# Queries and new keys of a paged attention turned by VectorE and spread by SBUF transfers, with two projections inside the output projection

## The chip, the core and the metric

The kernel runs on one core of a Trainium2 chip. A core has five engines with an instruction queue each: TensorE (PE: matmuls and, beside them, weight loads, PEld), VectorE (DVE), ScalarE (ACT), GpSimd (POOL) and SyncE (SP), which computes nothing and issues transfers. Sixteen DMA engines move what SP, ACT and POOL issue. The metric is the time of one execution in microseconds (us). The kernel before took 2267.02 us, the median of three runs (2259.68, 2267.02 and 2267.82).

## The reference, cut to what matters

There are 64 batches of 32 tokens with 512 features, all in float32. First each batch is mixed by one of 16 small matrices; then comes an attention with 32 query heads and 8 key heads of 128 features, over 512 cached keys (16 pages of 32 through a block table) and the 32 new keys.

```python
x = x + einsum('bct,bcd->bdt', x, weights[condition])
q = rope(rmsnorm((x @ Wq.T).reshape(64, 32, 32, 128)) )   # k likewise with 8 heads, v without
k_all, v_all = concat(cache[block_table], new)            # 512 + 32 keys
scores = q @ k_all / sqrt(128), masked past cache_seqlens
out = x + softmax(scores) @ v_all @ Wo.T
```

## The kernel before

**Tiles and steps.** Four batches make a tile of 128 tokens, so there are `NT` = 16 tiles. The heads are done in two halves (`NHH` = 2) of 4 key heads and 16 query heads. A step is one half of the heads of one tile: 32 steps, 0 to 15 for the first half (the text calls them first-half steps) and 16 to 31 for the second. The first half computes the mixed tile x1, turns it and stores it to memory with the partial result; the second half loads both again (`x1_a`, L337 to L345). `ahead` is the step after the one in work: its projections are made during the step in work.

**Slots.** A step runs over 4 batches times 4 key heads, that is 16 slots (`slot = bt * GH + g`, L864). A slot holds `scores` of this head (8 weight loads and matmuls of a 128 x 512 block, L534, then an exponential on ACT, L542) and `values` of the head before (L592), whose results DVE adds to the part of the new keys and divides (L604, L606, L607). At slot 0 stand `new_scores` (L545) and at slots 1 and 3 `new_values` (L562). At slot 3 stands the output projection of the step before, `out_proj` (L475), 16 matmuls of 128 x 512 after all slots of that step have gone through DVE's `turn` (L614). Which pieces for `ahead` stand in which slot is the table `pieces` (L822): `x1_a` at 0, the key projection `k_a` and the first query projection at 4, and so on.

**Projection, norm and turn.** `project` (L394) makes four matmuls for a 128 x 512 block. `norm_rope` (L402) squares it on ACT, sums on DVE, takes the power -0.5 on POOL, and multiplies and adds on DVE up to L433. The block then has tokens on the partitions, but the scores need features there, so `transposed` (L438) turns it by four TensorE transposes into PSUM, and ACT copies it out (`q_b`, L466; `k_b`, L451).

**Cached keys and values.** `load_k` (L272) brings the keys of one batch: SP first loads the 16 page numbers into registers (L278) and then issues 16 transfers of 64 KB (L286). There are two buffers, so the load for the batch two ahead waits until `head_keys` (L521) has copied the last head out of the buffer. `head_keys` is a DVE copy (L527), one a slot, a batch ahead of its use. Values come by indirect transfers of POOL (L310), four a batch, and ACT masks them (L323).

**Order.** SP and PE run their instructions in the order of the program (`manual_schedule`, L88). The order of DVE, ACT and POOL is set at build time by a planner, which goes by readiness in its own model. Every engine waits at the head of its queue. On SP this order is: the load for the batch two ahead at the top of each batch (slots 0, 4, 8 and 12), then what the pieces of the slots issue; at slot 0 of a step with a second-half `ahead` these are `acc` and `x1t` (L343, L345), behind the key load of slot 0. The buffer of `x1t` is single, and so is that of `nv`, the part of the new keys.

Of the kernel before, what the change touches and what calls it, by code (L numbers as in the profile page):

```python
# [11 lines left out]
F32 = mybir.dt.float32  # L12
# [7 lines left out]
P = 128  # L20
# [35 lines left out]
def cond_resid_paged_attention_kernel(  # L56
# [64 lines left out]
    sin = const.tile([P, NT, HD], F32, tag="sin", name="sin")  # L121
    half_pi = const.tile([P, 1], F32, tag="half_pi", name="half_pi")
    minus_half = const.tile([P, GH], F32, tag="minus_half", name="minus_half")
    rden = const.tile([P, NHH * NT * BT, GH], F32, tag="rden", name="rden")

    def positions():
        nc.vector.memset(half_pi, math.pi / 2)
# [58 lines left out]
    def steps_of(exact, pools):  # L186
# [15 lines left out]
        else:  # L202
# [10 lines left out]
        ]  # L213
        vn_bufs = [
            wpool.tile([P, GH, D + 1], F32, tag=f"vn{i}", name=f"vn{i}_{uid}")
            for i in range(2)
        ]

# [112 lines left out]
        class Step:  # L331
            def __init__(self, n):
                self.n, self.hh, self.t = n, n // NT, n % NT
                self.name = f"{n}_{uid}"
                self.qt = {}

        def x1_a(st):  # L337

# [60 lines left out]
                )  # L399
            return pp  # L400

        def norm_rope(st, pp, name, kind):  # L402

            cw, sw = st.rot[kind]
            p4 = pp.rearrange("p (h e f) -> p h e f", h=4, e=2)
            sq = work.tile([P, 4, D], F32, tag="w2", name=f"sq_{name}", bufs=1)
            nc.scalar.activation(  # L407
                sq.rearrange("p h d -> p (h d)"), pp, AF.Square, scale=1.0 / math.sqrt(D)
            )
            ms = small.tile([P, 4], F32, tag="ms", name=f"ms_{name}")  # L410
            nc.vector.tensor_reduce(ms, sq, AX.X, ALU.add)  # L411
            nc.vector.tensor_scalar_add(ms, ms, EPS)  # L412
            rs = small.tile([P, 4], F32, tag="rs", name=f"rs_{name}")
            nc.gpsimd.tensor_tensor(rs, ms, minus_half, ALU.pow)  # L414

            r = work.tile([P, 4, 2, HD], F32, tag="w1", name=f"rope_{name}")
            u = work.tile([P, 4, 2, HD], F32, tag="w2", name=f"ropeu_{name}", bufs=1)
            nc.vector.tensor_tensor(  # L418
                r.rearrange("p h e f -> p h (e f)"),
                pp.rearrange("p (h d) -> p h d", h=4),  # L420
                cw.rearrange("p e f -> p (e f)").unsqueeze(1).to_broadcast([P, 4, D]),
                ALU.mult,
            )
            for e in range(2):
                nc.vector.tensor_tensor(
                    u[:, :, e, :],
                    p4[:, :, 1 - e, :],
                    sw[:, e, :].unsqueeze(1).to_broadcast([P, 4, HD]),
                    ALU.mult,
                )  # L430
            nc.vector.tensor_tensor(r, r, u, ALU.add)
            rd = r.rearrange("p h e f -> p h (e f)")
            nc.vector.tensor_tensor(  # L433
                rd, rd, rs.unsqueeze(2).to_broadcast([P, 4, D]), ALU.mult
            )
            return rd

        def transposed(rd, name):  # L438
# [2 lines left out]
                nc.tensor.transpose(pt[:, h, :], rd[:, h, :], ident)  # L441
            return pt

        def k_a(st):
            if st.n > 1 or exact:
                rot_tables(st)
            name = f"k_{st.name}"
            pp = project(st, wt["k", st.hh, 0], f"pp_{name}")
            st.k_rope = norm_rope(st, pp, name, "k")

        def k_b(st):  # L451
            pt = transposed(st.k_rope, f"k_{st.name}")
            st.kn = act.tile([P, GH, P], F32, tag="kn", name=f"kn_{st.name}")
            nc.scalar.copy(st.kn, pt)

        def v_a(st):
            pp = project(st, wt["v", st.hh, 0], f"pp_v_{st.name}")
# [2 lines left out]

        def q_a(st, g):
            name = f"q_{st.name}_{g}"
            pp = project(st, wt["q", st.hh, g], f"pp_{name}")
            st.qt[g] = norm_rope(st, pp, name, "q")

        def q_b(st, g):  # L466
            pt = transposed(st.qt[g], f"q_{st.name}_{g}")
            qt = act.tile([P, BT, REP, S], F32, tag=f"qt{g}", name=f"qt_{st.name}_{g}")
            nc.scalar.copy(  # L469
                qt.rearrange("p b h s -> p h b s"),  # L470
                pt.rearrange("p h (b s) -> p h b s", b=BT),
            )
            st.qt[g] = qt

        def out_proj(st, halfway=None):  # L475

            po = ps_p.tile([P, HID], F32, tag="pp", name=f"pout_{st.name}")
            for i in range(QH):
                if halfway and i == 3 * QH // 4:
                    halfway()  # L480
                nc.tensor.matmul(  # L481
                    po,
                    st.ot[:, i, :],
                    wt["o", st.hh, i // 4][:, i % 4, :],
                    start=(i == 0),
                    stop=(i == QH - 1),
                )
            nc.vector.tensor_tensor(st.acc, po, st.acc, ALU.add)  # L488
            if exact or st is steps[-1]:
                store(st)  # L490
# [25 lines left out]
                    mask_ones(self.b)  # L516

        def queries(ba, g):
            return ba.st.qt[g][:, ba.bt].rearrange("p h s -> p (h s)")

        def head_keys(ba, g, eng=None):  # L521

# [22 lines left out]
        def new_scores(st):  # L545


            ps = ps_p.tile([P, GH, P], F32, tag="pp", name=f"psn_{st.name}")
            for g in range(GH):
                for bt in range(BT):  # L550
                    own = slice(bt * S, (bt + 1) * S)
                    nc.tensor.matmul(  # L552
                        ps[own, g, :],
                        st.kn[:, g, own],
                        st.qt[g][:, bt].rearrange("p h s -> p (h s)"),
                        start=True,
                        stop=True,
                    )
            st.pn = work.tile([P, GH, P], F32, tag="pn", name=f"pn_{st.name}", bufs=1)
            nc.scalar.activation(st.pn, ps, AF.Exp, scale=SCALE)  # L560
# [25 lines left out]
        def values(ba, g):  # L586
# [14 lines left out]
            if g % 2:  # L601
                both = slice(g - 1, g + 1)
                t = ba.st.nv[:, ba.bt, both, :]
                nc.vector.tensor_tensor(t, ba.po, t, ALU.add)  # L604
                rd = rden[:, ba.n, both]
                nc.vector.reciprocal(rd, t[:, :, D])  # L606
                nc.vector.tensor_tensor(  # L607
                    ba.o[:, both, :],
# [14 lines left out]
        def exact_batch(ba, key_no):  # L623
# [7 lines left out]
            for g in range(GH):  # L631
# [6 lines left out]
                nc.tensor.matmul(  # L638
                    ps[:, L:LK],
                    q,  # L640
                    st.kn[:, g, bt * S : (bt + 1) * S],
                    start=True,
                    stop=True,
                )
# [41 lines left out]
        if exact:  # L686
# [7 lines left out]
            for st in steps:  # L694
# [10 lines left out]
                x1_a(st)  # L705
                x1_c(st)
                x1_b(st)
                k_a(st)
                k_b(st)
                v_a(st)  # L710
# [39 lines left out]
        lens_at = work.tile([P, B], I32, tag="pr", name="lens_at", bufs=3)  # L750
        nc.gpsimd.dma_start(lens_at, lens_row.partition_broadcast(P))
        positions()
        trig = work.tile([P, 3, TRIG * HD], F32, tag="w1", name="trig0")
        angles(0, trig)
        for i in range(BT):
            blk = slice(i * S, (i + 1) * S)
# [9 lines left out]
        cached_rows(pages_at, lens_at)  # L766
        nc.vector.memset(vn_bufs[0][:, :, D : D + 1], 1.0)
        nc.vector.memset(vn_bufs[1][:, :, D : D + 1], 1.0)
        trig = work.tile([P, 3, TRIG * HD], F32, tag="w1", name="trig1")
        angles(TRIG, trig)  # L770
        for c in range(RAW):
            fetch(0, c)
# [49 lines left out]
        def pieces(st):  # L822
            do = {
                0: (x1_a,),
                4: (k_a, (q_a, 0)),
                5: ((q_a, 1),),
                6: (v_a, k_b, (q_b, 0)),
                8: ((q_a, 2), (q_b, 1)),
                10: ((q_a, 3), (q_b, 2)),
                13: ((q_b, 3),),  # L830
            }
            if st is second:
                do[4], do[6] = ((q_a, 0),), (k_b, (q_b, 0))
            return do

        valued, turned = (batch, GH - 1), batch
        new_ot(first)
# [14 lines left out]
        for st in steps:  # L852
# [4 lines left out]
            for bt in range(0 if st.n else 1, BT):  # L857
# [5 lines left out]
                for g in range(GH):  # L863
# [16 lines left out]
                    if slot == 3:  # L880
                        if ahead:
                            x1_b(ahead)
                        out_proj(steps[st.n - 1])
                        if st.n + 1 < NT // TRIG:
                            tmp = work.tile([P, 3, TRIG * HD], F32, tag="w1", name=f"trig_{st.n}")
                            with tc.issue_after(last["dve"]), tc.issue_after(last["act"]):
                                angles((st.n + 1) * TRIG, tmp)
                    if slot == 5 and st.n:
                        store(steps[st.n - 1])
                    if slot == 6 and 0 < st.n and st.n + 2 < NT:  # L890
# [25 lines left out]


        def in_range():
            rd = rden.rearrange("p n g -> p (n g)")
            good = work.tile([P, NHH * NT * BT * GH], F32, tag="w1", name="good")  # L920
            nc.vector.tensor_scalar(good, rd, DEN_LOW, None, ALU.is_ge)
            nc.vector.scalar_tensor_tensor(good, rd, DEN_HIGH, good, ALU.is_le, ALU.mult)
            count = small.tile([P, 1], F32, tag="ms", name="count")
            nc.vector.tensor_reduce(count, good, AX.X, ALU.add)
            ones = small.tile([P, 1], F32, tag="rs", name="ones")
            nc.vector.memset(ones, 1.0)
            pc = ps_p.tile([1, 1], F32, tag="pp", name="pcount")
            nc.tensor.matmul(pc, count, ones, start=True, stop=True)
            nc.vector.tensor_scalar(
                redo, pc, float(P * NHH * NT * BT * GH), None, ALU.not_equal  # L930
            )

        out_proj(steps[-1], in_range)

    redo = const.tile([1, 1], I32, tag="redo", name="redo")
    run(False)
# [54 lines left out]
```

## Time and profile before

| | |
|---|---|
| median of three runs | 2267.02 us |
| profiled execution, its own time | 2258.59 us |
| its span, first to last instruction | 2256.8 us |
| granted TensorE clock, mean | 0.997 |
| busy PE / PEld / DVE / ACT / POOL | 2223.5 / 1565.7 / 1076.0 / 940.4 / 779.8 us |
| DMA moved | 318.13 MB, mean 141 GB/s |
| TensorE transposes of queries and keys (L441) | 640 matmuls |
| issues of cached keys on SP (L286) | 2048 |

The page gives a busy time for each engine and a row for each group of equal instructions; a busy engine is not always the bound, and only the chain of work that ended last says what set the end. SP computes nothing, and so has no busy row; its issues are read from its timeline. In the text, s is the start of slot 0 of a step on PE.

### The profile page before, as it was taken

What the parts mean: (1) busy time and instruction counts of PE and PEld (TensorE: products, weight loads), DVE (VectorE), ACT (ScalarE), POOL (GpSimd) and SP (SyncE); (2) the same over time, 40 slices, a digit from 0 to 9 for tenths busy, and PEclk for the clock granted to TensorE, in tenths of its full rate; (3) what the DMA queues carried; (4) which work ended last, traced back from release to release, by engine and by line L of the source; (5) the groups of instructions that cost most, each with busy time, mean ns of one, the idle gap of its engine ahead of it and who ended that gap; (6) DMA issues with size and microseconds to landing.
All of it is one profiled execution on the core that took longest, in us unless ns stands there. A gap on an engine that the chain in (4) does not pass through costs nothing.

```text
span 2256.8 us, 41920 instructions
## 1 busy us (share of the span) xinstructions
PE 2223.5 (99%) x13590; PEld 1565.7 (69%) x13590; DVE 1076.0 (48%) x2722; ACT 940.4 (42%) x1724; POOL 779.8 (35%) x1008
## 2 busy tenths in 40 slices
PE   8999999999999999999999999999999999999998
PEld 5767677676776677766777666777666777666775
DVE  5545455443554444543545544455444455444452
ACT  3534454444433444433444333443334443343442
POOL 4423333233433333332333333333323343233331
PEclk9999999999999999999999999999999999999999
DMA  7744544345443455435756444553344544444542
GB/s 229 195 131 128 154 134 128 114 128 154 142 121 113 130 152 155 116 113 157 229 168 169 124 137 138 154 148 115 115 145 139 160 124 127 124 130 151 159 116 74
DMA packets 364053, 318.13 MB, mean 141 GB/s; under 512 B 46800, under 2 KB 308960, under 8 KB 363824
## 3 DMA queue, kind: packets, MB, share of 16 engines
q1 hardware_dynamic: 319104, 174.44, 27.0%
q0 software_dynamic: 41712, 136.66, 20.4%
q10 hardware_dynamic: 3008, 4.25, 0.5%
q8 instruction: 110, 1.80, 0.3%
q14 instruction: 119, 0.97, 0.1%
HBM read 302.59 MB, written 12.58 MB: 140 GB/s over the span
## 4 chain that ended last, share of the span: by engine, by line
PE 90%; DMA 4%; DVE 2%; issue 2%; SPq 2%; ACT 1%; POOL 1%; ACTq 0%; DVEq 0%; POOLq 0%
PE pout_x L481 19%; PE pp_q_x L397 19%; PE po_x L592 18%; PE ps_x L534 18%; PE pp_k_x L397 5%; PE pp_v_x L397 5%; PE pt_q_x L441 2%; PE pnv_x L576 2%; DMA raw_x<-in_vc_dram,v_row 2%; SPq L286 1%; PE psn_x L552 1%; DMA k_t_x<-in_kt_dram 1%; PE pt_k_x L441 1%; PE pmix_x L353 1%; DMA pages_at<-in_pages_v_dram 0%
## 5 line engine op out<-in xcount | busy, mean ns | idle before, releaser
L310 POOL DMA_INDIRECT raw_x<-in_vc_dram,v_row x512 | 515.0, 1006 | 718.6 <-ACT v_x L323 659.3
L542 ACT ACTIVATE pr_x<-ps_x 128x512 f32<-128x512 f32 x512 | 305.4, 600 | 628.3 <-PE ps_x L534 624.8
L592 PE MATMUL po_x<-v_x,pr_x 128*128 128x129 f32 x4096 | 551.9, 278 | 5.6 <-ACT pr_x L542 5.6
L534 PE MATMUL ps_x<-qt_x,kh_x 128*128 128x128 f32 x4096 | 542.1, 275 | 2.8 <-DVE kh_x L527 2.2
L592 PEld LDWEIGHTS po_x<-v_x,pr_x 128*128 128x128 f32 x4096 | 503.1, 192 | 49.5 <-issue 30.4
L534 PEld LDWEIGHTS ps_x<-qt_x,kh_x 128*128 128x128 f32 x4096 | 502.8, 192 | 27.3 <-issue 19.8
L397 PE MATMUL pp_q_x<-wq_x,x1t_x 128*128 128x512 f32 x1024 | 463.7, 596 | 3.3 <-ACT qt_x L469 3.3
L481 PE MATMUL pout_x<-wo_x,ot_x 128*128 128x512 f32 x1024 | 445.0, 592 | 0.0
L323 ACT ACTIVATE v_x<-raw_x,valid 128x512 f32<-128x512 f32 x512 | 362.6, 724 | 114.4 <-DMA raw_x<-in_vc_dram,v_row 113.9
L481 PEld LDWEIGHTS pout_x<-wo_x,ot_x 128*128 128x128 f32 x1024 | 192.2, 190 | 229.0 <-issue 228.7
L397 PEld LDWEIGHTS pp_q_x<-wq_x,x1t_x 128*128 128x128 f32 x1024 | 188.4, 192 | 203.8 <-issue 200.1
L527 DVE COPY kh_x<-k_t_x 128x512 f32<-128x512 f32 x506 | 213.2, 424 | 108.8 <-DMA k_t_x<-in_kt_dram 68.2
L407 ACT ACTIVATE sq_q_x<-pp_q_x 128x512 f32<-128x512 f32 x128 | 76.4, 597 | 306.5 <-issue 135.4
L411 DVE TENSOR_REDUCE ms_q_x<-sq_q_x 128x4 f32<-128x512 f32 x128 | 87.4, 682 | 200.0 <-ACT sq_q_x L407 200.0
L414 POOL TENSOR_TENSOR rs_q_x<-ms_q_x,minus_half 128x4 f32<-128x4 f32 x128 | 132.9, 1038 | 132.7 <-DVE ms_q_x L412 132.7
L604 DVE TENSOR_TENSOR nv_x<-po_x,nv_x 128x258 f32<-128x258 f32 x256 | 107.7, 421 | 146.9 <-PE po_x L592 138.7
L386 POOL TENSOR_TENSOR cw_k_x<-norm_k,cos 128x64 f32<-128x64 f32 x32 | 10.1, 315 | 382.7 <-DVE ms_k_x L412 382.7
L418 DVE TENSOR_TENSOR rope_q_x<-pp_q_x,cw_q_x 128x512 f32<-128x512 f32 x128 | 87.3, 682 | 103.4 <-PE pt_k_x L441 103.4
L488 DVE TENSOR_TENSOR xt_x<-pout_x,xt_x 128x512 f32<-128x512 f32 x16 | 11.1, 692 | 246.6 <-PE pout_x L481 246.6
L488 DVE TENSOR_TENSOR acc_x<-pout_x,acc_x 128x512 f32<-128x512 f32 x16 | 11.1, 692 | 220.7 <-PE pout_x L481 220.7
L397 PE MATMUL pp_v_x<-wv_x,x1t_x 128*128 128x512 f32 x256 | 115.2, 593 | 0.0
L397 PE MATMUL pp_k_x<-wk_x,x1t_x 128*128 128x512 f32 x256 | 115.2, 593 | 0.0
(99 smaller groups left out, 1575.7 us busy)
## 6 DMA issues: line engine op xcount, KB each, us to landing
k_t_x<-in_kt_dram SPq DMA_DIRECT2D x2048, 64.0 KB
raw_x<-in_vc_dram,v_row POOLq DMA_INDIRECT x512, 4.0
wo_x<-in_wo_dram SPq DMA_DIRECT2D x32, 256.0 KB
xt_x<-in_x_dram SPq DMA_DIRECT2D x16, 256.0 KB
x1t_d<-x1t_x ACTq DMA_DIRECT2D x16, 256.0 KB
acc_d<-xt_x SPq DMA_DIRECT2D x16, 256.0 KB
wq_x<-in_wq_dram SPq DMA_DIRECT2D x8, 512.0 KB
acc_x<-acc_d SPq DMA_DIRECT2D x16, 256.0 KB
```

Of the source, the lines that this page charges most:

```text
L310: nc.gpsimd.indirect_dma_start(out=raw.rearrange("p g d -> p (g d)"), out_offset=None, in_=vc, in_offset=bass.IndirectOffsetOnAxis(ap=v_ro ...
L323: nc.scalar.activation(v_bufs[b % 2][:, c, :, 0:D], raw, AF.Copy, scale=ok)
L397: nc.tensor.matmul(pp, st.x1t[:, c, :], w[:, c, :], start=(c == 0), stop=(c == KC - 1))
L411: nc.vector.tensor_reduce(ms, sq, AX.X, ALU.add)
L414: nc.gpsimd.tensor_tensor(rs, ms, minus_half, ALU.pow)
L418: nc.vector.tensor_tensor(r.rearrange("p h e f -> p h (e f)"), pp.rearrange("p (h d) -> p h d", h=4), cw.rearrange("p e f -> p (e f)").uns ...
L481: nc.tensor.matmul(po, st.ot[:, i, :], wt["o", st.hh, i // 4][:, i % 4, :], start=(i == 0), stop=(i == QH - 1),)
L527: last["dve"] = nc.vector.tensor_copy(k, ba.k_raw[:, :, g, :]).ins
L534: nc.tensor.matmul(ps[:, c, :], ba.k[g][:, c * P : (c + 1) * P], queries(ba, g), start=True, stop=True,)
L542: last["act"] = nc.scalar.activation(pr, ps, AF.Exp, scale=SCALE).ins
L592: nc.tensor.matmul(ba.po[:, g % 2, :], ba.pr[g][:, c, :], ba.v_t[:, c, g, :], start=(c == 0), stop=(c == VC - 1),)
L604: nc.vector.tensor_tensor(t, ba.po, t, ALU.add)
```

## The change

The queries and new keys are no longer turned by TensorE after step 0. `turn_rows` has DVE transpose the blocks of 32 x 32, which leaves each block's features on the 32 partitions of its batch; the piece `spread` then has SP issue 16 transfers within SBUF (4 batches times 4 blocks of features, each 32 partitions of 2560 bytes) that bring each block to its own partitions. The queries and keys of a step lie together in `rows`; each transfer takes all five of them and so waits for the last query. The columns of batches 0 to 2 have one buffer, those of batch 3 have two. The projections of the keys and of the first query group now stand inside the output projection, after its 4th and its 8th matmul; the other projections move up in the slots. The tables of the rotation are made at slot 2. The check of the denominators (`rden`) is made once for each half of the heads. The buffer `w1` becomes single.

```diff
+        rows = wpool.tile([P, 4, GH + 1, P], F32, tag="rows", name=f"rows_{uid}")
+        q_cols = wpool.tile([P, BT - 1, GH + 1, P], F32, tag="q_cols", name=f"q_cols_{uid}")
+        q_last = [
+            wpool.tile([P, GH + 1, P], F32, tag=f"q_last{i}", name=f"q_last{i}_{uid}")
+            for i in range(2)
+        ]
...
+        def turn_rows(st, i, rd, name):
+            nc.vector.transpose(
+                rows[:, :, i, :].rearrange("p k (h s) -> p h k s", h=4),
+                rd.rearrange("p h (k d) -> p h k d", k=4),
+            )
+        def columns(st, bt):
+            return q_last[st.n % 2] if bt == BT - 1 else q_cols[:, bt]
+        def spread(st, batches):
+            for bt in batches:
+                for k in range(4):
+                    nc.sync.dma_start(
+                        columns(st, bt)[k * S : (k + 1) * S, :, :],
+                        rows[bt * S : (bt + 1) * S, k, :, :],
+                    )
+        def by_tensor(st):
+            return st.n == 0 or exact
+        def finish(st, i, pp, name, kind):
+            if by_tensor(st):
+                norm_rope(st, pp, name, kind, rows[:, :, i, :])
+            else:
+                turn_rows(st, i, norm_rope(st, pp, name, kind), name)
+        def to_columns(st, i):
+            pt = transposed(rows[:, :, i, :], f"{i}_{st.name}")
+            p4 = pt.rearrange("p h (b s) -> p b h s", b=BT)
+            n = BT - 1
+            nc.scalar.copy(q_cols[:, :, i, :].rearrange("p b (h s) -> p b h s", h=4), p4[:, 0:n])
+            nc.scalar.copy(
+                columns(st, n)[:, i, :].rearrange("p (h s) -> p h s", h=4), p4[:, n]
+            )
...
-        def out_proj(st, halfway=None):
+        def out_proj(st, between={}):
             po = ps_p.tile([P, HID], F32, tag="pp", name=f"pout_{st.name}")
             for i in range(QH):
-                if halfway and i == 3 * QH // 4:
-                    halfway()
+                if i in between:
+                    between[i]()
...
         def queries(ba, g):
-            return ba.st.qt[g][:, ba.bt].rearrange("p h s -> p (h s)")
+            return columns(ba.st, ba.bt)[:, g, :]
...
             do = {
                 0: (x1_a,),
-                4: (k_a, (q_a, 0)),
-                5: ((q_a, 1),),
-                6: (v_a, k_b, (q_b, 0)),
-                8: ((q_a, 2), (q_b, 1)),
-                10: ((q_a, 3), (q_b, 2)),
-                13: ((q_b, 3),),
+                2: (rot_tables,),
+                4: ((q_a, 1),),
+                5: (v_a,),
+                6: ((q_a, 2),),
+                8: ((q_a, 3),),
+                10: ((spread, (0, 1, 3)),),
+                11: ((spread, (2,)),),
             }
...
                     if slot == 3:
                         if ahead:
                             x1_b(ahead)
-                        out_proj(steps[st.n - 1])
+                        between = {}
+                        if ahead:
+                            between[REP] = lambda: k_a(ahead)
+                            between[2 * REP] = lambda: q_a(ahead, 0)
+                        out_proj(steps[st.n - 1], between)
...
+                    if slot == GH and st.n == NT:
+                        count(0)
```

## The prediction

> **What bounds the kernel now.** I read the page's busy shares first, then the chain that ended last, then one step of it (the second-half step that begins at 1571.95), and at last the queues of SP, DVE and ACT in that step.
>
> ```profile
> PE 2223.5 (99%) x13590; PEld 1565.7 (69%) x13590; DVE 1076.0 (48%) x2722; ACT 940.4 (42%) x1724; POOL 779.8 (35%) x1008
> ...
> PE 90%; DMA 4%; DVE 2%; issue 2%; SPq 2%; ACT 1%; POOL 1%; ACTq 0%; DVEq 0%; POOLq 0%
> ```
>
> TensorE is the bound nearly everywhere; what leaves it is gained, and what makes it wait is lost. The chain prices the work that leaves:
>
> ```profile
> 1567.05 0.44 PE pt_q_x L441 x4
> ...
> 1580.26 1.31 PE pnv_x L576 x15
> 1581.57 1.09 PE po_x L592 x8
> 1582.66 13.73 PE pout_x L481 x32
> ```
>
> Four transposes (with their four loads) take 0.437 us. The third line's wait is small but telling: the same `pnv` takes 0.66 us elsewhere. Its cause is seen on DVE and ACT:
>
> ```profile
> 1574.98 0.43 DVE L604 TENSOR_TENSOR nv_x<-po_x,nv_x 128x258 f32<-128x258 f32 x1 [3.35 <-PE po_x L592]
> 1578.55 0.43 DVE L527 COPY kh_x<-k_t_x 128x512 f32<-128x512 f32 x1 [3.14 <-DMA k_t_x<-in_kt_dram]
> ...
> 1579.09 0.42 DVE L607 TENSOR_TENSOR o_x<-nv_x,rden 128x256 f32<-128x256 f32 x1
> ...
> 1579.60 1.21 ACT L584 COPY nv_x<-pnv_x 128x258 f32<-128x258 f32 x4 [3.07 <-DVE o_x L607]
> ```
>
> The key copy waits 3.14 us at the head of DVE for a late key load; behind it the old `nv` is read late, so ACT may not overwrite it, the PSUM tiles of `new_values` stay full, and PE waits 0.65 us. So key loads already arrive at the limit at the start of a step. SP says why:
>
> ```profile
> 1549.18 9.26 SPq L286 DMA_DIRECT2D k_t_x<-in_kt_dram  x16
> ...
> 1565.55 9.66 SPq L286 DMA_DIRECT2D k_t_x<-in_kt_dram  x16
> ...
> 1585.56 0.43 SPq L343 DMA_DIRECT2D acc_x<-acc_d  x1
> 1586.09 0.38 SPq L345 DMA_DIRECT2D x1t_x<-x1t_d  x1
> ```
>
> The loads of slots 8 and 12 each need over 9 us of SP to issue; the load of slot 0 follows at once (first issue 1576.55, after its 1.0 us load of page numbers, L278) and ends at 1585.5; only then comes `x1t`. One issue costs SP about 0.52 us, gap included, also where the address is fixed and 32 partitions are moved:
>
> ```profile
> 1211.65 4.05 SPq L239 DMA_DIRECT2D wo_x<-in_wo_dram  x8
> ```
>
> (4.05 - 0.43) / 7 = 0.52. The only pause of SP near here is 1558.4 to 1565.55, before the load of slot 12.
>
> **What the Trainium skill says.** "DMA: Bandwidth & Descriptors", section "Issuing engines are not separate DMA queues", calls the sequencer's time to initiate a DMA "usually small relative to the DMA itself". Here it isn't: 16 issues of 64 KB take 8.3 us, so SP brings at most 1.05 MB / 8.3 us = 126 GB/s this way. "SBUF — State Buffer", section "Door 1: The DMA port swizzle", measures 189 GB/s for 32 partitions, an estimate of 1.31 MB / 189 = 6.9 us for the spread, less than its issue time; no trace of before has such a transfer. "TensorE: Matmul & The Clock Gate", Part 1, halves the clock after an idle window of about 3.4 us. The start of this trace agrees: after PE's gap from about 25 to 29 us the granted clock falls.
>
> ```profile
> 24.00:28.00 4.00, 0.89 (x5) 1.00 1.02 380
> 28.00:32.00 4.00, 3.00 (x4) 0.68 1.05 391
> 32.00:36.00 4.00, 4.00 (x19) 0.89 0.78 245
> ```
>
> (Columns: stretch and its length, PE busy, clock, DMA share, GB/s.) One such gap costs 4 x 0.32 + 4 x 0.11 = 1.7 us.
>
> **The change, part by part.**
>
> *Gain on PE.* Transposes go in 31 of 32 steps: 31 x 5 x 0.437 = 67.7 us, 2.18 us a step. The projections only move; their 3.44 us each stay.
>
> *DVE.* 155 block transposes at the 0.71 us of `turn`'s row (L617, same 128 x 512): 110 us on an engine at 48%, so hidden as work; its latency counts below. The write is strided, so 0.7 to 1.0 us. ACT loses 5 copies of 0.59 us a step, worth nothing as it waits 625 us for PE. Tables at slot 2, the single `w1`, and the two checks of `rden` (about 1 us of DVE each) are covered by PE's slots; uncovered they cost a microsecond once or so. Step 0 gains five more ACT copies, at most 2 us once.
>
> *When the rows are ready.* The last query projection now stands in slot 8. From its end to s are values (0.89) and seven slots of 1.79 us: 13.4 us. Its chain on ACT, DVE and POOL took 4.9 us in the step shown (projection end 1561.25 to the end of L433 at 1566.13); with 0.71 the rows are ready at s - 7.8.
>
> *The spread on SP.* 16 x 0.52 = 8.3 us, to s + 0.5 (bounds: 0.33 us for the instruction alone, 5.3 us; with the slow issues of the key loads at 0.6, 9.6 us). It cannot use SP's pause: slots 8 to 11 shrink to 10.6 us, the slot-8 load ends at about s - 8.4, and the rows come just then. The last transfer lands about 1.7 us after its issue (as `x1t` did: 1586.09 to the next issue, which waits for it, 1587.79), at s + 1.8; `new_scores` wants it at s + 0.9: a stall of 0.9.
>
> *What is behind it on SP.* The key load of slot 12 begins at s - 6.4 now (1565.55 against 1571.95). Behind the spread and the page load (1.3 with its gap) it begins at s + 1.9: 8.3 us later. Behind it, all 8.3 us later, are the load of slot 0 and `x1t`.
>
> - Second-half `ahead`, 16 steps: `x1t` was issued at s + 14.1, now at s + 22.4, and lands at s + 24.1. PE wants it after the fourth matmul of the output projection, no longer after the sixteenth: s + 10.1 (its start without the 0.65 stall) + 3.4 = s + 13.5. Stall 10.6; net 10.6 - 0.65 - 2.18 = +7.8 a step, +124 us.
> - The other 15 step starts: the key copy's wait ended at s + 5.3 in the first-half step that starts at 949.1, with 0.6 us to spare before PE; 8.3 later it stalls PE by 7.7, if DVE's order stays. The planner puts what it believes ready first, so it may put divisions and `turn` ahead of the late copy; then only the 0.9 remains. I take 6: the copy was planned at least 3.1 us too early in the step shown, so the planner is too sure of SP, and a copy behind the division still holds up the mix of x1 (`x1_c`). Net 6 - 2.2 = +3.8, +57 us (bounds +83 and -19).
>
> Sum: 2258.6 (the profiled execution's own time; span 2256.8) + 124 + 57 = 2440. That execution lies 8.4 us under the median and within the runs' 8 us of spread, more or less; I add half, 2445.
>
> **Rivals.**
> 1. *DVE re-planned.* The copies stand behind everything urgent; only `x1t` stalls: 2258.6 + 124 - 19 = 2364, with the offset 2370. For it: it needs no luck but the planner's. Against: the order of before.
> 2. *The clock falls too.* Stalls of 8 to 10 us are longer than the gap at 25 us; 31 x 1.7 = 53 on top of the fully blocked 2466: about 2520. For it: the clock row above. Against: waits may be broken into pieces by single slots.
> 3. *Faster: the spread fits into SP's pause.* If rows come early enough, or issues are cheap enough, that the slot-12 load begins at most x later, then second-half steps cost 1.8 + x - 2.83 (even unmoved, `x1t`, issued on average 3.0 us after the output projection began, comes 1.2 us after PE's new wish, 1.8 with the stall removed) and the others at most 0.9 - 2.2 or x - 0.6 - 2.2. Break-even is at x = 1.9 us; at x = 0 the time is 2258.6 - 16 - 19 = 2223, or 2230. For it: SP waits 663 us for key copies in all. Against: x is 8.3 by the rows, and even with all 16 issued at the bare 0.33 it is 5.3.
> 4. *DMA or DVE as the bound.* 1.31 MB on some 9.9 MB a step; slices up to 229 GB/s are on the page, and DVE would be at about half. No time of its own.
>
> **Chances.** Likeliest case (`x1t` and part of the DVE stalls, 2400 to 2500): 0.58; rival 1 and things near it (2330 to 2400): 0.23; rival 2 (above 2500): 0.12; rival 3: 0.05; within 0.5% (a chance cancellation): 0.02. Half a per cent, about 11 us, is what a measurement of this kernel can tell from no change. So faster 0.05, same 0.02, slower 0.93. The range 2340 to 2525 leaves out the faster cases and the tails of rivals 1 and 2.
>
> **What would show it.** Right: in the changed profile SP shows two runs of 12 and 4 spread issues ending near s, PE waits inside the output projection before the key projection in steps 15 to 30 for `x1t` by about 10 us, and key copies on DVE wait over 8 us at a step's start; PE's share falls to some 88%; no L441 after step 0. Wrong: spread issues far below 0.5 us, rows ready long before the slot-8 load ends, or `x1t` landing before s + 15.

## The result, and the profile after

The changed kernel takes 2614.28 us (median; 2605.06 to 2621.94) where the kernel before takes 2267.31 beside it: a ratio of 1.1538, 95% interval 1.1488 to 1.1587. It is slower, as forecast, but by 347 us instead of 178, and 2614 lies outside the range of 2340 to 2525.

The page of the changed kernel, first the busy time of each engine, then the granted clock in 40 slices, then the chain that ended last by engine and by line:

```profile
PE 2285.0 (87%) x12970; PEld 1582.6 (60%) x12970; DVE 1184.9 (45%) x2881; ACT 886.7 (34%) x1586; POOL 768.8 (29%) x1008
...
PEclk9899999999999999998889889988999889988899
...
PE 64%; SPq 19%; DMA 8%; issue 5%; DVE 2%; ACT 0%; POOL 0%; ACTq 0%; another core or an unknown queue 0%; POOLq 0%; DVEq 0%
PE pout_x L520 15%; PE pp_q_x L406 15%; PE po_x L631 11%; PE ps_x L573 11%; SPq L296 10%; SPq L470 7%; PE pp_k_x L406 6%; PE pp_v_x L406 4%; DMA q_cols_x<-rows_x 3%; DMA x1t_x<-x1t_d 3%; PE psn_x L591 1%; SPq L288 1%; PE pnv_x L615 1%; DMA wo_x<-in_wo_dram 1%; DMA wq_x<-in_wq_dram 1%
```

TensorE issues 620 matmuls fewer (31 steps x 5 x 4 transposes), and yet its busy time rises from 2223.5 to 2285.0. Its share falls from 99% to 87%, and the clock line, all nines before, has eights: one near the start, the others from the middle on, where the second half of the heads begins. SP's issuing, 2% of the chain before, is 19% now.

From the busy times it can be worked out where the time went. Take busy time as the work of before plus what slower matmuls add, and the rest of the span as idle:

| | span | PE busy | PE idle | busy beyond the work |
|---|---|---|---|---|
| before | 2256.8 | 2223.5 | 33.3 | |
| after | 2617.3 | 2285.0 | 332.3 | 129.2 |

The work of after is 2223.5 - 67.7 = 2155.8 (the transposes at 0.437 us for four are gone), so 2285.0 - 2155.8 = 129.2 us of busy time go beyond the work. Then +299.0 idle, +129.2 slow matmuls and -67.7 transposes make +360.5, the difference of the spans; as the 129.2 is what was left over, this balance closes by itself. The record of the granted clock in the trace tests it: it holds 1.0 or 0.5 and nothing between, TensorE was busy for 232.7 us at 0.5, and half of that, 116 us (5 before), was lost. So some 111 of the 129 us are the clock; the other 18 stay unexplained. Below, "slow clock" is the time beyond the work.

The list of waits of after names the idle time (engine, line, what it waited for: us in total, times, longest):

```profile
PE psn_x L591 <- DMA q_cols_x<-rows_x: 151.9, 34, 9.0
PE pp_k_x L406 <- DMA x1t_x<-x1t_d: 125.1, 16, 10.0
...
PEld psn_x L591 <- DMA q_cols_x<-rows_x: 43.9, 11, 5.0
```

There are two waits: `new_scores` for the spread columns at the steps' starts, and the key projection for `x1t` in each of the 16 second-half steps. (The weight load's row overlaps the first in part.) One second-half step, which starts at 1445.0, shows both. The timeline of SP (start, us from first to last issue, count):

```profile
1430.12 6.23 SPq L296 DMA_DIRECT2D k_t_x<-in_kt_dram  x12
1436.82 5.26 SPq L470 DMA_DIRECT2D q_cols_x<-rows_x  x8
1442.13 2.49 SPq L470 DMA_DIRECT2D q_last_x<-rows_x  x4
1444.72 2.43 SPq L470 DMA_DIRECT2D q_cols_x<-rows_x  x4
1448.48 18.64 SPq L296 DMA_DIRECT2D k_t_x<-in_kt_dram  x32
1467.17 0.43 SPq L352 DMA_DIRECT2D acc_x<-acc_d  x1
1467.64 0.43 SPq L354 DMA_DIRECT2D x1t_x<-x1t_d  x1
```

The sixteen issues run from s - 8.2 to s + 2.2. The key load of slot 12, which began at s - 6.4 before, begins at s + 3.5, and `x1t` is issued at s + 22.6. TensorE and VectorE in that step:

```profile
1451.19 0.60 PE L591 MATMUL psn_x<-q_cols_x 128*32 128x128 f32 x2 [4.77 <-DMA q_cols_x<-rows_x]
1472.69 5.13 PE L406 MATMUL pp_k_x<-wk_x,x1t_x 128*128 128x512 f32 x8 [6.88 <-DMA x1t_x<-x1t_d]
```

```profile
1460.50 0.43 DVE L646 TENSOR_TENSOR o_x<-nv_x,rden 128x256 f32<-128x256 f32 x1
1460.87 1.44 DVE L566 COPY kh_x<-k_t_x 128x512 f32<-128x512 f32 x4
```

TensorE waits 4.77 and 6.88 us; the key projection behind the second wait takes 5.13 us instead of 3.44. The key copies stand behind the division now and wait for nothing. The clock by stretches (stretch and length; PE, PEld, DVE, ACT, POOL busy; clock; DMA share; GB/s):

```profile
1445.00:1448.33 3.33, 1.42 (x14) 1.03 (x12) 0.43 (x1) 1.69 (x3) 0.91 (x2) 1.00 0.93 251
1448.33:1455.15 6.82, 3.96 (x37) 3.51 (x38) 0.00 (x0) 1.32 (x2) 1.01 (x2) 0.50 0.79 209
1455.15:1468.81 13.66, 10.66 (x89) 7.91 (x88) 4.13 (x11) 6.72 (x15) 3.58 (x5) 1.00 0.51 141
1468.81:1475.63 6.82, 2.94 (x4) 1.42 (x5) 0.00 (x0) 0.00 (x0) 0.45 (x1) 0.50 0.76 250
...
1445.00:1529.30 84.30, 71.81 (x414) 49.51 (x412) 36.55 (x88) 27.17 (x49) 23.57 (x32) 0.92 0.46 131
```

The step before, in the same columns:

```profile
1503.40:1571.95 68.55, 68.55 (x422) 48.48 (x422) 32.71 (x82) 28.08 (x53) 23.87 (x31) 1.00 0.45 135
```

Each of the two waits halves the clock for 6.82 us, and 3.96 and 2.94 us of them fall on matmuls after the wait. In the whole run 50 of the 51 stretches at half clock last a whole multiple of 3.41 us, 28 of them 6.83. The whole step, the last line of the first list, takes 84.3 us against 68.55 before: 12.5 idle, and 71.8 busy where the work is 68.55 - 2.18 = 66.4, so 5.4 of slow clock; 12.5 + 5.4 - 2.2 = 15.7. A first-half step (832.07 to 908.12) takes 76.05 against 70.47: 5.0 idle, the rest clock.

### The profile page after: what moved, and what is told of

Read it like the earlier page. It is cut to its first block, busy times and chain, and to the rows that moved or that the text cites. A ratio compares the mean times of both kernels' runs of the same rounds, so it can differ in the third digit from the quotient of the medians.

```text
span 2617.3 us, 41594 instructions
## 1 busy us (share of the span) xinstructions
PE 2285.0 (87%) x12970; PEld 1582.6 (60%) x12970; DVE 1184.9 (45%) x2881; ACT 886.7 (34%) x1586; POOL 768.8 (29%) x1008
## 4 chain that ended last, share of the span: by engine, by line
PE 64%; SPq 19%; DMA 8%; issue 5%; DVE 2%; ACT 0%; POOL 0%; ACTq 0%; another core or an unknown queue 0%; POOLq 0%; DVEq 0%
PE pout_x L520 15%; PE pp_q_x L406 15%; PE po_x L631 11%; PE ps_x L573 11%; SPq L296 10%; SPq L470 7%; PE pp_k_x L406 6%; PE pp_v_x L406 4%; DMA q_cols_x<-rows_x 3%; DMA x1t_x<-x1t_d 3%; PE psn_x L591 1%; SPq L288 1%; PE pnv_x L615 1%; DMA wo_x<-in_wo_dram 1%; DMA wq_x<-in_wq_dram 1%
## 5 line engine op out<-in xcount | busy, mean ns | idle before, releaser
L631 PE MATMUL po_x<-v_x,pr_x 128*128 128x129 f32 x4096 | 581.2, 287 | 15.2 <-POOL v_x L336 12.9
L631 PEld LDWEIGHTS po_x<-v_x,pr_x 128*128 128x128 f32 x4096 | 532.6, 200 | 99.3 <-issue 71.2
L573 PE MATMUL ps_x<-q_cols_x,kh_x 128*128 128x128 f32 x3072 | 419.6, 281 | 13.7 <-DMA q_cols_x<-rows_x 13.3
L573 PEld LDWEIGHTS ps_x<-q_cols_x,kh_x 128*128 128x128 f32 x3072 | 393.0, 199 | 38.0 <-issue 36.0
L406 PE MATMUL pp_k_x<-wk_x,x1t_x 128*128 128x512 f32 x256 | 152.7, 752 | 125.1 <-DMA x1t_x<-x1t_d 125.1
L423 POOL TENSOR_TENSOR rs_q_x<-ms_q_x,minus_half 128x4 f32<-128x4 f32 x128 | 131.0, 1024 | 299.4 <-DVE ms_q_x L421 299.4
L591 PE MATMUL psn_x<-q_cols_x 128*32 128x128 f32 x768 | 77.2, 388 | 160.8 <-DMA q_cols_x<-rows_x 151.9
L420 DVE TENSOR_REDUCE ms_k_x<-sq_k_x 128x4 f32<-128x512 f32 x32 | 22.0, 686 | 406.1 <-ACT sq_k_x L416 406.1
L406 PEld LDWEIGHTS pp_k_x<-wk_x,x1t_x 128*128 128x128 f32 x256 | 61.4, 248 | 213.0 <-issue 213.0
L336 POOL COPY v_x<-valid 128x16 f32<-128x16 f32 x128 | 27.9, 218 | 549.5 <-PE po_x L631 538.4
L591 PEld LDWEIGHTS psn_x<-q_cols_x 128*32 128x32 f32 x768 | 48.5, 150 | 176.5 <-issue 129.0
```

The source lines that it names most:

```text
L406: nc.tensor.matmul(pp, st.x1t[:, c, :], w[:, c, :], start=(c == 0), stop=(c == KC - 1))
L573: nc.tensor.matmul(ps[:, c, :], ba.k[g][:, c * P : (c + 1) * P], queries(ba, g), start=True, stop=True,)
L591: nc.tensor.matmul(ps[own, g, :], columns(st, bt)[:, GH, g * S : (g + 1) * S], columns(st, bt)[:, g, :], start=True, stop=True,)
L631: nc.tensor.matmul(ba.po[:, g % 2, :], ba.pr[g][:, c, :], ba.v_t[:, c, g, :], start=(c == 0), stop=(c == VC - 1),)
```

## The experiments

My theory after the result: SP's sixteen issues and their landing come late; what stands behind them on SP is late by as much; and each gap lets the clock fall. The rivals: it is the bytes rather than the issues; it is the moved projections, which want `x1t` sooner; it is the place of the spread in SP's order, which a better place would cure. Each kernel differs from the changed kernel by what is shown or named.

**e1, `x1t` a step earlier.**

```diff
-                0: (x1_a,),
+                0: () if st.hh else (x1_a,),
...
+                    if slot == 11 and NT <= st.n + 2 < len(steps):
+                        x1_a(steps[st.n + 2])
```

> The changed kernel, but the loads of acc and x1t for a second-half step are issued one step earlier, at slot 11 right behind the spread and ahead of the key load of slot 12. Theory (everything behind the spread on SP is late, and x1t is late the most): the waits of the key projection for x1t (125 us in all) go, and with them the slow matmuls after the gap (about 2 us each in 16 steps); the wait of new_scores for the spread stays. About 2617 - 125 - 32 = 2460 us. Rival (the projections inside the output projection cost by themselves, or DVE's transposes do): the time stays above 2560, as another wait takes the place of this one.

Measured: 2454.3 us, ratio 1.0835 (1.0804 to 1.0867). The wait for `x1t` is gone. Span 2454.3, busy 2244.7: idle 209.6, slow clock 88.9. So the late `x1t` costs 160 us; of the 163 between the two spans, 123 are idle time and 40 are clock.

**e3, the two projections back in slot 4**, behind the whole output projection; the rest as changed.

```diff
-                4: ((q_a, 1),),
-                5: (v_a,),
-                6: ((q_a, 2),),
+                4: (k_a, (q_a, 0)),
+                5: ((q_a, 1),),
+                6: (v_a, (q_a, 2)),
...
-                            between[REP] = lambda: k_a(ahead)
-                            between[2 * REP] = lambda: q_a(ahead, 0)
```

> The changed kernel with the key projection and the first query projection back at slot 4 behind an undivided output projection; the last query projection stays at slot 8 and the spread as it is. Theory: x1t is wanted 10.3 us later and no longer waited for, the wait for the spread stays: about 2460 us as with the early x1t. Rival (the place of the projections doesn't matter, the late queue costs what it costs): no change from 2614.

Measured: 2449.4 us, 1.0814 (1.0779 to 1.0848). The same wait is removed from its other end, and the same time comes back. e1 and e3 are within 5 us of each other, so in the changed kernel the moved projections cost nothing beyond their earlier wish for `x1t`.

**e4, the moves alone**: TensorE's transposes in every step (slots 12 to 15), no block transpose and no spread.

```diff
-            return st.n == 0 or exact
+            return True
...
-                10: ((spread, (0, 1, 3)),),
-                11: ((spread, (2,)),),
+                12: ((q_b, 0), k_b),
+                13: ((q_b, 1),),
+                14: ((q_b, 2),),
+                15: ((q_b, 3),),
```

> The moved projections alone: TensorE turns queries and keys in all steps as in the kernel before (at slots 12 to 15, since the column buffers of batches 0 to 2 are in use until slot 11), no DVE transposes of queries and keys, no spread. Theory: x1t, which already landed about 4 us after its issue at s + 14 in the kernel before, is now wanted at s + 13.5, so 16 steps wait some 4 to 5 us and lose 1 to 2 us to the slow clock behind it: 2267 + 90 = 2355 us; first-half steps as before. Rival (the moved projections are free): 2267 within 1 per cent.

Measured: 2321.6 us, 1.0249 (1.0137 to 1.0361), from two runs 21 us apart: the moves, with the smaller changes that e4 keeps, make the kernel slower, by some 2.5% where I expected 3.9%. TensorE waits for `x1t` here too, without any spread: 34.0 us in 11 steps, of 53 us of added idle time. Even without late issues `x1t` comes just behind the earlier wish. The same with `x1t` a step earlier was not run.

**e8, fillers in the gap**: e1 with 20 matmuls of the identity ahead of `new_scores`.

```diff
                    if slot == 0:
+                        if st.n:
+                            keep_warm(20)
                         new_scores(st)
```

> The kernel with the early x1t, with 20 matmuls of the identity (4.4 us at full clock) put before new_scores in every step, where PE waits for the spread. Nothing is left out. Theory (the gap makes the clock fall and the matmuls behind it run slow, 1.5 us a step): the gap is filled, the clock stays, about 2454 - 45 = 2410 us. Rival (the clock costs nothing of note): 2454 or a little more.

Measured: 2410.3 us, 1.0642 (1.0621 to 1.0663), as expected, clock 0.989 instead of 0.955: 44 us less with more work issued. The 31 x 20 fillers are two matmuls each in the trace; these 1240 take 0.112 us each at full clock (8 of that shape in 0.893), an estimate of 138 us. Busy time is 2325.1, so real work took 2187, 31 beyond 2155.8 where e1 had 89; idle fell from 210 to 83. Filling costs 138 - 126 = 12 us and saves 58 of slow clock. By the clock's own record the loss falls from 77 to 20 us. This shows that the clock, and not the wait alone, takes time.

**e5 and e6, bytes against issues**, both on e1. The columns that they leave out keep old values.

```diff
-                for k in range(4):
+                for k in range(2):
```

(e6. e5 keeps the four, each with two of the five row blocks:)

```diff
-                        columns(st, bt)[k * S : (k + 1) * S, :, :],
-                        rows[bt * S : (bt + 1) * S, k, :, :],
+                        columns(st, bt)[k * S : (k + 1) * S, 0:2, :],
+                        rows[bt * S : (bt + 1) * S, k, 0:2, :],
```

> The kernel with the early x1t, whose spread carries only the first 2 of the 5 blocks of rows: 16 issues as before, but 32 KB each, 0.52 MB a step instead of 1.31 MB. What is left out is the columns of two query groups and of the new keys; they keep stale values. Theory (the number of issues is the cost, about 0.63 us each on SP): the wait of new_scores shrinks only by what landing shortens, 1 to 2 us a step: 2454 - 45 = about 2410 us. Rival (the bytes are the cost, on the DMA engines): the wait of some 6 us a step goes, below 2300 us.

> The kernel with the early x1t, whose spread carries whole rows, but only the first 2 of the 4 blocks of features: 8 issues of 80 KB, 0.66 MB a step. What is left out is half of the features of all queries and new keys; they keep stale values. Theory (issues): 8 x 0.63 = 5 us less on SP before the last lands, so the wait of new_scores nearly goes and the slow clock behind it too: 2454 - 190 = about 2265 us, well below the run with fewer bytes. Rival (bytes): no better than the run with fewer bytes, which moves less.

Measured: e5 2366.9 us, 1.0450 (1.0426 to 1.0474), between the theory and the rival; e6 2259.7, 0.9989 (0.9978 to 1.0000), as expected. The traces tell the two apart. In e5 the sixteen issues take as long as in e1 (medians of 10.5 and 10.2 us, both at a spacing of 0.63), but the last transfer lands 1.6 us after its issue instead of 3.5 in e1. In e6 the eight issues take 5.0 us, and the last lands after 3.5 us as in e1. By these readings e5's 87 us come from the landing, and e6's 195 from the issues. An estimate for the least that the issues can be worth: if bytes counted in proportion, half of them would be worth 73 of the 195, and halving the issues 122. Both count, issues more. The list of waits of e6:

```profile
PE psn_x L591 <- DMA q_cols_x<-rows_x: 17.1, 11, 5.8
```

With half of the features unmoved, half of a spread fits: the wait of e1 (159.5 us) is nearly gone, and the 68 us of the transposes only just pay for what is left.

**e2, the sixteen issues from ACT's queue.**

```diff
-                    nc.sync.dma_start(
+                    nc.scalar.dma_start(
```

> The changed kernel with the 16 transfers of the spread issued by ACT instead of SP. Theory (SP's queue): the key load of slot 12 begins at s - 6.4 again, x1t lands some 10 us earlier and the wait for it nearly goes; the wait of new_scores for the spread itself stays near 5 us a step, since 16 issues in a row take as long from ACT. About 2400 us. Rival (the bytes of the spread fill the DMA engines, or DVE's transposes are the cost): the same bytes move at the same time, so the time stays within 2 per cent of 2614. A third: ACT is held by the issues, exponentials come late, and the time is no better than 2550.

Measured: 2652.1 us, 1.1709 (1.1675 to 1.1743). My theory's 2400 failed, and the third outcome named there came. ACT in one step:

```profile
1507.43 7.23 ACTq L470 DMA_DIRECT2D q_cols_x<-rows_x  x8
1515.13 2.89 ACTq L470 DMA_DIRECT2D q_last_x<-rows_x  x4
1518.14 3.25 ACTq L470 DMA_DIRECT2D q_cols_x<-rows_x  x4
1521.72 0.72 ACT L333 ACTIVATE v_x<-raw_x,valid 128x512 f32<-128x512 f32 x1 [14.11 <-DMA k_t_x<-in_kt_dram]
```

Values and exponentials stand behind the issues for 14.1 us. The issues themselves are 16 x 0.56 = 9; the rest is waiting. In this program the transfers of SP and ACT signal on eight completion semaphores in turn, and an issue waits until the earlier transfer on its semaphore has landed, here key loads of SP's queue, as the bracket says. (In the trace every transfer of the two names one of eight semaphores, and waits for the same one.)

**e7, through memory**: the rows written to memory with one issue at slot 7 and read back transposed by 4 + 4 issues (ACT at slot 9, SP at slot 11); the queries of groups 0 and 1 and the keys projected within the output projection, groups 2 and 3 in slots 4 and 5; `x1t` as in e1.

```diff
+        def put(st):
+            nc.sync.dma_start(rows_d[st.n % 2], rows.rearrange("p k i c -> p k (i c)"))
...
+        def get(st, last_batch):
+            n = BT - 1
+            for k in range(4):
+                src = rows_d[st.n % 2].rearrange("(b p) k e -> k p b e", b=BT)[k]
...
-                10: ((spread, (0, 1, 3)),),
-                11: ((spread, (2,)),),
+                7: (put,),
+                9: ((get, True),),
+                11: ((get, False),),
```

> All lessons in one: x1t early; keys and the first two query groups inside the output projection, the other two at slots 4 and 5 and the values at slot 6, so the rows are ready some 16 us ahead of the next step; the rows go to memory with one transfer and come back with 4 issues on ACT (batch 3) and 4 on SP (batches 0 to 2) instead of 16 on SP. Theory (only SP's issues and lateness cost): no wait of over 1 us remains for the columns, and the 67 us of transposes become a gain: 2200 to 2240 us, faster than before. Rival (a transposition by DVE and transfers always ends in a new wait, here ACT held by its issues or the key loads): above 2267 us.

Measured: 2610.7 us, 1.1539 (1.1513 to 1.1566), far from the 2200 to 2240 expected. Fewer issues did not help: one of them waits at the head of the queue, and the read lands late. SP's own waits, and its timeline in a step that starts at 1077.0:

```profile
SPq L470 <- DVE rows_x L460: 286.3, 23, 14.0
```

```profile
1059.65 0.35 SPq L470 DMA_DIRECT2D rows_d_x<-rows_x  x1
1063.25 12.76 SPq L300 DMA_DIRECT2D k_t_x<-in_kt_dram  x16
1076.30 2.37 SPq L482 DMA_DIRECT2D q_cols_x<-rows_d_x  x4
```

SP waits up to 14 us at the write for the last rows; the key load of slot 8 comes behind it, at s - 13.8 instead of s - 22.8 as before; the read comes behind that, at s - 0.7, and its last packet lands 9.5 us later. TensorE waits 9.76 us for it. The key load takes 12.76 us to issue here, as its issues also wait for ACT's reads on the shared semaphores (87.3 us over the run, 29 times). What the wait at the head, these waits and the landing are worth each was not separated.

**e10 and e11, the spread ahead of the key load.** Projections and `x1t` as in e7, spread within SBUF as in the change, batches 3, 0 and 1 at slot 7; batch 2 from ACT at slot 13 (e10) or from SP at slot 11 (e11).

```diff
-                4: ((q_a, 1),),
-                5: (v_a,),
-                6: ((q_a, 2),),
-                8: ((q_a, 3),),
-                10: ((spread, (0, 1, 3)),),
-                11: ((spread, (2,)),),
+                4: ((q_a, 2),),
+                5: ((q_a, 3),),
+                6: (v_a,),
+                7: ((spread, (3, 0, 1)),),
+                13: ((spread, (2,)),),
```

> Nothing is left out. Against the changed kernel: the loads of x1 are issued a step early as in e1; queries of groups 0 and 1 and the new keys are projected within the output projection, groups 2 and 3 at slots 4 and 5, the values at slot 6; the spread of batches 3, 0 and 1 (12 issues) stands at slot 7, ahead of the key load of slot 8 on SP's queue, and that of batch 2 (4 issues) is issued by ACT at slot 13. Theory (the cost is that the spread trails the last key load and so lands after the step's end, with the loads behind it and the clock falling in the gaps): no wait for the columns is left and the whole gain of the transposes shows. From e4, which has the moved projections but TensorE's transposes (2322): 2322 - 68 for the transposes - 34 for its waits on x1 = 2220, between 2200 and 2260, granted clock 0.98 or more. Rival (16 issues of SP and ACT cost what they cost wherever they stand, 10 us of a step's queue, so key loads come late in place of the columns): 2350 to 2450 with waits for key loads in the waits list.

> As e10, but the four issues of batch 2 stay on SP at slot 11, behind the key load of slot 8. Theory: these four end about 4 x 0.63 = 2.5 us after the last of that key load and land 3.3 us later, about 5 us after the start of the next step, so new_scores waits some 3 us at each of 30 starts: e10 + 60 to 130 (with the clock that such a gap costs), 2290 to 2350. Rival (the place of the issues does not matter): within 15 us of e10.

Measured: e10 2530.9 us, 1.1182 (1.1160 to 1.1204); e11 2476.9, 1.0946 (1.0926 to 1.0967). The theory failed twice: no better than e1, and e10 above e11 though I had it below. The wait has moved from the columns to the keys. SP in e11, in the step that starts at 1426.7, then TensorE and VectorE at its start:

```profile
1410.14 2.44 SPq L470 DMA_DIRECT2D q_last_x<-rows_x  x4
1412.69 5.04 SPq L470 DMA_DIRECT2D q_cols_x<-rows_x  x8
1419.28 10.16 SPq L296 DMA_DIRECT2D k_t_x<-in_kt_dram  x16
1429.54 2.44 SPq L470 DMA_DIRECT2D q_cols_x<-rows_x  x4
```

```profile
1434.33 2.05 PE L573 MATMUL ps_x<-q_cols_x,kh_x 128*128 128x128 f32 x8 [7.67 <-issue]
```

```profile
1433.81 1.43 DVE L566 COPY kh_x<-k_t_x 128x512 f32<-128x512 f32 x4 [7.80 <-DMA q_cols_x<-rows_x]
```

The last rows are ready at s - 16.5, and until then SP waits (300.1 us over the run, 24 times, for `rows` alone). The columns come in time now, but the key load behind the first twelve issues begins at s - 7.4 instead of s - 22.8, its last issue comes after the step's start, and the first scores stall for these keys: the bracket of TensorE names nothing, but VectorE copies the keys only at 1433.81, and the scores start behind the first of these copies. (Its bracket names the columns, which share semaphores with the keys; the copy reads keys alone.) In e10 batch 2 from ACT puts its landing on the shared semaphores, and SP's key load waits for it (49.6 us, up to 4.8); that this is the whole difference of 54 us was not tested.

**e12 and e13, the issues from POOL.** As e11, with all sixteen from POOL; those of batch 2 at slot 12; in e13 the twelve of slot 7 stand in fours at slots 7, 8 and 9.

```diff
-                    nc.sync.dma_start(
+                    nc.gpsimd.dma_start(
```

> As e11 (projections and loads of x1 early, batches 3, 0 and 1 spread at slot 7), but all 16 issues of the spread come from POOL, those of batch 2 at slot 12; nothing is left out. Theory (SP's queue has no room: the key loads of slots 8, 12 and 0 stand back to back on it, so ten microseconds of other issues make key loads late wherever they stand, which e10 and e11 showed): with SP free of the spread, the waits for the keys at the step's start go, 2200 to 2300, clock 0.98 or more. Rival (the transfers themselves and their semaphores cost, on whatever queue, or POOL's own issue of about 1 us each holds up the fetches of values behind it): 2400 or more, with POOL's fetches and ACT's copies of values late.

> As e12, but the twelve issues of batches 3, 0 and 1 stand in fours at slots 7, 8 and 9 with POOL's fetches of values between them, instead of all at slot 7; nothing is left out. Theory (what is left in e12 is that 6 to 8 us of issues in one piece hold up the fetches of values, which ACT and then the products with the values wait for, some 110 us in the waits): 2290 to 2350, with the waits on the values down by half or more. Rival (the fetches are late because POOL has 16 x 0.52 = 8.3 us more work per step in all, or their data share the DMA engines with the spread): within 25 us of e12, 2355 to 2400.

Measured: e12 2377.6 us, 1.0522 (1.0504 to 1.0539); e13 2367.7, 1.0444 (1.0421 to 1.0467). Taking the issues off SP is worth 99 us against e11 (whose last four stand one slot earlier), so that much of e11's loss was SP's order; but it does not reach the 2200 to 2300 of the theory. In e12 the columns hold TensorE for 5.7 us in all. The list of waits of e12 shows what came in their place:

```profile
ACT v_x L333 <- DMA raw_x<-in_vc_dram,v_row: 212.4, 127, 10.7
...
PE po_x L631 <- ACT v_x L333: 113.2, 80, 11.0
```

The products with the values wait for ACT's copies, and these for the fetches that POOL issues (113.9 us before). Breaking the piece in fours, which I expected to halve this, left it (255.6 and 108.8 us), and the time came out as the rival named there had it. Whether POOL's 16 x 0.5 us or the spread's share of the DMA engines makes the fetches late was not separated.

No version ran faster than the kernel before by more than can be told; e6, which leaves out half of the spread, is level with it.

## Why the prediction was wrong in size

By its own steps, in the order of its sum:

- *Gain on PE, 67.7 us.* Right in the count: 620 matmuls fewer. Their price was not measured by itself in the changed kernel.
- *Rows ready at s - 7.8.* Right: VectorE's last block transpose ends at 1436.76, s - 8.2.
- *The spread on SP, 8.3 us to s + 0.5.* Short. The median spacing of spread issues is 0.63 us, not the 0.52 that I worked out from the weight loads (from start to start these have a median of 0.47), and the sixteen take 10.3 us. The upper bound of 9.6 was too low.
- *Landing 1.7 us after the issue.* Misread. I took SP's pause behind `x1t` for its landing; it is SP's load of page numbers (L278, 1.0 us) with its gaps. By the packets in the traces the last spread transfer lands 3.3 us after its issue (median; 2.4 to 4.2 in 29 of 31 steps), and `x1t` 4.6 (4.4 before). This and the slower issues make the stall of 4.8 us at `new_scores` instead of 0.9.
- *What is behind it on SP.* Right in mechanism: `x1t` issued at s + 22.6 (predicted s + 22.4). That the time is so near is partly luck, as the key loads ahead of it began 1.6 us later than predicted and were issued faster, 32 in 18.64 us. Its wait is 6.9 us in the step shown, not 10.6, as TensorE was held up before it by the other stall and the slow clock.
- *The key copies on DVE, 6 us in the other 15 steps.* Wrong. VectorE's order was planned anew, the copies stand behind the division, and rival 1 was right in this. A stall of 5.0 us came all the same, but from the columns; that it is near the 6 is luck.
- *The sum.* The working has 16 x (10.6 - 0.65) + 15 x 6 = 249 us of added idle time; 299 was measured. That this is near is cancellation: `x1t` took 125 (170 in the working), the key copies nothing that TensorE saw (90), and the columns some 174 (none; 151.9 in the row shown and 22 in two smaller ones). It has nothing for the clock; 129 was measured. 50 + 129 = 179, and 2440 + 179 = 2619, the time of the profiled execution.

So the step that failed is the pricing of a stall at its length alone, which put the clock at nothing where 129 us were measured; beside it the wait for the columns, 0.9 us a start, was about five times too small. The fall of the clock stood beside the sum as rival 2, with 0.12 and 1.7 us a step. Its objection, that waits might be broken into pieces, did not hold: there are 31 + 16 = 47 whole gaps, and 129.2 / 47 = 2.7 us each (2.4 by the clock's record). The Trainium skill, "TensorE: Matmul & The Clock Gate", Part 1, which the prediction cited, also says that the clock comes back only after about 3.4 us of sustained work. The windows above agree roughly (a clock of 0.50 for 3.96 and 2.94 us of work after the two gaps, 1.00 between), and a k projection of 5.13 us instead of 3.44 shows what one re-warming cost there; the gap at 25 us, short and at the start, had shown too little of it.

The case with this price and both idle terms as I had them gives 2440 + 129 = 2569, outside my range as well; the other 50 us are the net of the idle terms. With the 50 alone, at 2490, it would have been inside.

The Trainium skill, "DMA: Bandwidth & Descriptors", section "Issuing engines are not separate DMA queues", calls the time of initiating usually small, and says that starting transfers from several engines saves only that time. One issue is small here too, 0.59 us against 3.3 to its landing. But sixteen stand in a row while their landings overlap, 10.3 us before the last 3.3, and this kernel is the case that the "usually" leaves out (half of the issues gone: 122 us at least, by the estimate above; all moved off SP: 99 us).

## What to carry to other kernels

Before adding transfers to an in-order queue, write down what stands behind them and by when each is wanted: of the 347 us here 160 were in a load that the transfers pushed back (e1), beside the wait for the transfers themselves, and the other places tried in the same queue only changed what was late. Price a stall of TensorE of the lengths seen here (4 to 20 us) as its length plus 2 to 3 us of slow matmuls. Take the landing time of a transfer from its packets, never from the next instruction of the queue that issued it.

## What was not expected of the hardware

- Gaps of 4 to 20 us cost about the same clock whatever their length: 2.7 us for each of 47 gaps in the changed kernel, 2.9 in e1 (88.9 / 31, gaps near 5 us), 2.6 in e7 (81.1 / 31, most gaps of 8 to 20), 2.3 in e10 (70.0 / 30). By the clock's record it is nearer still, 2.2 to 2.3 us for each stretch at half clock (116 / 51, 77 / 34, 82 / 38 and 75 / 34). In e5, with gaps near 3 us, it is 2.1 (55 / 26), and some of the gaps left the clock whole.
- An SP issue that moves 32 partitions of 2560 bytes within SBUF took 0.63 us from one to the next (median), with 1024 bytes as well (e5); a read of 32 partitions from memory 0.47 (the weight loads of before, e7), a key load of 128 partitions 0.52, and more where it waits for a semaphore (e11: 10.16 us for 16). From POOL an issue of the spread took 0.49 to 0.55. Sixteen are 8 to 10 us of either queue.
- Eight completion semaphores shared by SP and ACT tie the two queues together: sixteen issues from ACT took 14.0 us where 9 were needed (e2).
